# A whole program ordered by count: layer 0's weight products planned behind the last scattered rows, nine counted durations corrected, new ranks

## The chip, the core and the metric

The kernel runs on one core of a Trainium2 chip. The core has engines that run their own instruction streams side by side: PE (TensorE, matmuls and transposes), DVE (VectorE), ACT (ScalarE), POOL (GpSimd) and SP (SyncE, which here only issues DMA transfers). They meet through semaphores. The metric is the device time of one execution in microseconds (us).

## What is computed

A transformer of four layers on 4 sequences ("rows") of 512 tokens with 128 features, in float32. Each layer has two half-weighted feed-forwards around an attention, and the same feed-forward weights are used twice:

```
x = x + 0.5 * ffn(layernorm(x))
x = x + attn(layernorm(x))
x = x + 0.5 * ffn(layernorm(x))
```

This change touches layer 0 most. Its feed-forward is a mixture of 8 experts, two per token, and one shared expert:

```
scores = softmax(xt @ gate_w.T)
_, idx = top_k(scores + gate_b, 2)
comb = (take_along_axis(scores, idx)[..., None] * one_hot(idx, E)).sum(1)
for each expert e:
    h = swiglu((xt @ w1[e] + b1[e]) * (xt @ w3[e] + b3[e]))
    routed += comb[:, e] * (h @ w2[e] + b2[e])
shared = swiglu((xt @ sw1 + sb1) * (xt @ sw3 + sb3)) @ sw2 + sb2
return routed + shared
```

Layer 0's attention has 16 heads of 64 with low-rank queries, keys and values and a rotary turn of queries and keys; its output is `out @ w_out.T + residual`. Layer 1's feed-forward mixes low-rank pairs of 8 experts by a gate taken from one token of each row, and its attention looks back over a window; here the window runs along the axis of the 4 rows. Layer 2 has a switch feed-forward (one expert per token, at most 64 tokens per expert and row) and causal attention with 16 heads of 8. Layer 3 has a feed-forward that mixes each token with the one before it, and full attention with 16 heads of 8.

## The kernel before

**How the order is made.** Every stage is written as Python generators ("processes"), one for each row, tile or head. A process yields a request before each piece of work: which engine, how many us it is counted at, which buffers it needs, which named events it waits for, and the earliest time. `run` keeps a counted clock for each engine. Again and again it takes the request that can start earliest; among requests of one engine that could start at nearly the same counted time, the process with the lowest number in the table RANK goes first. `any_of` and `moving` offer a choice of engines; the one that would be done first is taken, with an addition for dearer engines (DEARER0 until the second feed-forward of layer 0 has its buffers, DEARER after that, DEARER2 once the first heads of layer 2 begin). Where PE would idle in the count, `kept_warm` puts in junk matmuls on the identity (L1523). So the order of each engine's instructions is fixed when the program is built. On the chip nothing of the count remains: an engine takes its instructions in that order, and waits only for semaphores that follow from data, buffers and transfers.

**Layer 0's feed-forward, first time (0 to about 180 us).** Row by row, `route` finds the two experts of each token and the token's place among that expert's rows, which needs the counts of the rows before it. It then scatters the normalised tokens to these places in a table `sorted_x` in device memory: L631, on POOL, eight indirect DMAs for each row, 32 in all, each counted at 1.3 us. Its event `asent{b}` is the counted end of row b's last scatter plus 2.3 us. `weigh` (L643 to L650) makes the gate weights. Meanwhile PE has work that doesn't need the routing:

- `common`, the shared expert: L685 up-projections into PSUM, L1459 on ACT or DVE adds a bias, L692, L700, L705, L708, L710 and L717 form the gated value on DVE, ACT or POOL, L724 is the down-projection (16 matmuls on the profile for a row), and L728 on DVE adds it to x.
- `fold`: L738 makes room for the biases in each expert's weights, copied back by L1453. After the last, `folded` (L745, on SP) transfers the bias rows into that room.
- `l0_outputs`: two products L1199 of attention weights, 16 matmuls of 64 rows and 64 columns each in the profile, which read different quarters of the array, and L1203 (DVE) that copies them out. They are first needed in the attention, far later.

When all rows are routed, `plan` computes which tile of 128 rows belongs to which expert: L771 on POOL casts the experts' ends, L775 to L797 on DVE work out the tiles, eight transfers of zeros on SP (L803) fill up each expert's last tile, L809 on PE turns the plan and L812 on DVE makes it whole numbers, which SP and PE read into registers. `places` (L819 to L842, DVE) finds where each token's results will lie. Then `tiled` runs tile pairs of 128 rows: SP loads them (L868; the first load waits for all scatters and zero fills), PE transposes (L876), multiplies by the expert's weights (L887, two products), ACT, DVE and POOL form the gated value (L897, L907, L913, L918, L921, L923, L927), PE transposes and multiplies again (L935, L947), and SP stores (L955). `fetched` gathers each token's results (L977, indirect DMA on POOL).

**The rest.** Layer 0's attention (`l0_rotated` L1217 to L1235, `l0_scoring` L1250, `l0_weighing` L1265, `l0_valuing` L1289, `l0_adding` L1321 and L1323) runs from about 180 to 565 us. Then comes the feed-forward of layer 0 again (second tiles from about 616 us), without any folds or L1199, then layer 1 and layer 2's first feed-forward, and from about 866 us the heads of layers 2 and 3 (L2067 scores, L2083 exponentials, L2095 masks, L2109 values) with the remaining feed-forwards between them.

The line of `run` that picks the addition for a dearer engine:

```
dearer = DEARER2 if "begin0" in events else DEARER if "tiles" in events else DEARER0
```

Of the kernel before, what the change touches and what calls it, by code (L numbers as in the profile page):

```python
# [18 lines left out]
B, S, D = 4, 512, 128  # L19
# [21 lines left out]
def done(b):  # L41
# [12 lines left out]
RANK = {  # L54
    "adda": -1.39, "att0": -17.03, "att1": 2.6, "att2": -31.37, "att3": -27.46, "backa0": -27.3, "backa1": -39.8, "backa2": -37.75, "backa3": -3.37,
    "begin0": 15.63, "begin1": -9.44, "begin2": 13.19, "begin3": -8.46, "begin4": 19.37, "begin5": 46.26, "begin6": 17.84, "begin7": 38.68,
    "bringin": 46.21, "bringing": 8.27, "channels0": -7.83, "channels1": -48.04, "channels2": -33.98, "channels3": -10.84, "channels4": -83.4,
    "channels5": -55.2, "channels6": -6.12, "commona0": -2.18, "commona1": -1.54, "commona2": -13.4, "commona3": 3.84, "commonb0": -6.75,
    "commonb1": 13.93, "commonb2": 15.85, "commonb3": 20.13, "end0": 4.32, "end1": -19.31, "end2": -8.87, "end3": -33.5, "end4": -9.59, "end5": -8.7,
    "end6": 4.72, "expsa": 17.48, "fetching": -24.33, "first0": 1.49, "first1": 0.69, "first2": -7.74, "first3": 3.2, "fold0": -3.85, "fold1": 12.13,  # L60
    "fold2": -13.35, "fold3": -46.85, "fold4": -4.06, "fold5": -6.94, "fold6": -4.77, "fold7": 29.51, "folding": -79.59, "half0": -6.96,
    "half1": -4.34, "kept0": 10.41, "kept0.0": 3.74, "kept0.1": 2.38, "kept0.2": 10.73, "kept0.3": 1.02, "kept0.4": -0.44, "kept0.5": 22.23,
    "kept0.6": 24.57, "kept0.7": -10.37, "kept0.8": 40.73, "kept0.9": 48.22, "kept0.10": 23.18, "kept0.11": 9.99, "kept0.12": 0.6, "kept0.13": 9.71,
    "kept0.14": -22.33, "kept0.15": -0.06, "kept0.16": 2.86, "kept0.17": 26.78, "kept0.18": 2.62, "kept0.19": 8.71, "kept0.20": -18.45,
    "kept0.21": -13.79, "kept0.22": 42.98, "kept0.23": 8.44, "kept0.24": -2.84, "kept0.25": -21.29, "kept0.26": 38.94, "kept0.27": -18.06,
    "kept0.28": 1.29, "kept0.29": -19.57, "kept0.30": 23.52, "kept0.31": 27.06, "l1_ready": -33.26, "looked": 76.83, "looked0": 55.63,
    "looked1": 107.62, "looked2": 88.74, "looked3": 67.36, "looked4": 70.75, "looked5": 65.59, "looked6": 63.55, "masking": 17.37, "mix0": -33.39,
    "mix1": -15.62, "mix2": 1.56, "mix3": -50.5, "mix4": -23.7, "mix5": -27.69, "mix6": -55.99, "mix7": -30.78, "ones0": -43.5, "ones1": -12.11,
    "others": 28.89, "outputs": 8.15, "placesa": -10.15, "placesb": 45.04, "plana": 39.45, "planb": -6.79, "plus0": 7.25, "plus1": 30.99,
    "rot0": 5.7, "rot1": 16.46, "rot2": 26.99, "rot3": -2.01, "rot4": 0.1, "rot5": 2.62, "rot6": 4.73, "rot7": 11.49, "rot8": 40.56, "rot9": -12.44,  # L70
    "rot10": 17.51, "rot11": -39.23, "rot12": -37.85, "rot13": 15.54, "rot14": -7.75, "rot15": 5.5, "rot16": -3.26, "rot17": 14.91, "rot18": -2.48,
    "rot19": 0.55, "rot20": -6.7, "rot21": 6.92, "rot22": 7.74, "rot23": 12.78, "rot24": 15.52, "rot25": 0.78, "rot26": -4.58, "rot27": 6.38,
    "rot28": -0.8, "rot29": -2.7, "rot30": -8.6, "rot31": -12.59, "routea0": -6.93, "routea1": -3.77, "routea2": -4.6, "routea3": -82.97,
    "routeb0": -15.04, "routeb1": -20.66, "routeb2": -1.6, "routeb3.0": -35.7, "routeb3.1": -30.11, "scorea": 18.7, "scoring": 32.74, "send0": 4.01,
    "send1": -31.58, "send2": 14.86, "send3": 33.82, "send4": 40.53, "send5": 34.29, "send6": 59.05, "send7": 34.47, "start0": 7.62,
    "start1": -25.77, "start2": -5.21, "start3": 5.86, "take0": -6.04, "take1": -13.34, "take3": 22.16, "take5": 12.18, "take7": -1.16,
    "tilea0": -19.71, "tilea1": -16.33, "tilea2": -10.97, "tilea3": -11.39, "tilea4": -31.67, "tilea5": -23.9, "tilea6": -16.68, "tilea7": -15.26,
    "tilea8": -2.27, "tilea9": 8.62, "tilea10": -2.85, "tilea11": 11.3, "tilea12": 11.37, "tilea13": 26.86, "tilea14": -11.51, "tilea15": 17.87,
    "tilea16": 25.51, "tilea17": 8.65, "tilea18": -5.64, "tilea19": 15.81, "tileb0": -6.52, "tileb1": -26.02, "tileb2": -13.14, "tileb3": -7.5,
    "tileb4": -1.76, "tileb5": -15.98, "tileb6": -12.28, "tileb7": -4.02, "tileb8": 4.67, "tileb9": 6.74, "tileb10": 0.85, "tileb11": -0.27,  # L80
    "tileb12": 13.89, "tileb13": 16.56, "tileb14": 12.26, "tileb15": 9.35, "tileb16": 12.53, "tileb17": 14.26, "tileb18": 5.96, "tileb19": 25.99,
    "turning": 87.33, "valuea": -10.03, "values": 59.72, "watched0": 49.3, "watched1": 65.31, "watched2": 7.07, "watched3": 10.64, "weigha0": 56.46,
    "weigha1": 36.64, "weigha2": 27.13, "weigha3": 34.3, "weighb0": 42.98, "weighb1": -11.29, "weighb2": 6.67, "weighb3": 18.75, "weighing": 21.28,
    "whole_l2": 12.5, "whole_l3": 12.47, "zeroing": 59.35,
}
# [3 lines left out]
ARRIVALS = {"x0": 3.6, "x1": 4.5, "x2": 5.6, "x3": 6.6, "routing": 7.5, "common": 11.5, "w130": 16.5, "w131": 21.5, "aplace": 22.0, "bs": 22.5, "w2": 25.0, "b2": 25.5, "abase0": 0.0, "bbase0": 0.0, "ident": 8.0}  # L89
DEARER2 = {"PE": 0.0, "ACT": 0.2, "DVE": 0.5, "POOL": 0.2, "SP": 0.0}  # L90
DEARER = {"PE": 0.0, "ACT": 0.1, "DVE": 0.3, "POOL": 0.2, "SP": 0.0}
DEARER0 = {"PE": 0.0, "ACT": 0.0, "DVE": 0.3, "POOL": 0.5, "SP": 0.0}
# [192 lines left out]
def program(ctx: ExitStack, tc: tile.TileContext, a: dict, out: bass.AP, worst, verdict):  # L285
# [902 lines left out]
    def l0_outputs(w, pairs):  # L1188

        wvo = w["w_out"]  # L1190
        for h2 in range(2):
            yield PE(2.3, "big", wait=["pairs", "attn_w"])
            took("big")
            pw = big()
            for q in range(4):
                hp = 4 * h2 + q
                for u in range(2):
                    r = slice(64 * u, 64 * u + 64)
                    nc.tensor.matmul(pw[r, u, q * P : (q + 1) * P], lhsT=pairs[r, hp, :], rhs=w["w_out"][r, hp, :], start=True, stop=True)  # L1199
            yield DVE(1.3)  # L1200
            for u in range(2):
                r = slice(64 * u, 64 * u + 64)
                nc.vector.tensor_copy(wvo[r, 4 * h2 : 4 * h2 + 4, :].rearrange("p h d -> p (h d)"), pw[r, u, :])  # L1203
            free("big")

    def l0_rotated(n, w, head):

        b, hp = pairs0[n]
# [22 lines left out]
        for v, m, at in ((qk, 0, t0), (other, 1, None)):  # L1231
            yield DVE(1.15, at=at)
            nc.vector.tensor_tensor(v, v, rope[:, m, :].unsqueeze(1).to_broadcast([P, 2, S]), ALU.mult)
        yield DVE(1.15)
        nc.vector.tensor_tensor(qk, qk, other, ALU.add)  # L1235
# [72 lines left out]
    def l0_adding():  # L1308

        for n, (b, hp) in enumerate(pairs0):  # L1310
# [5 lines left out]
            for i in range(3):  # L1316
                half = (i + 1) // 2
                yield DVE(1.15, wait=[f"pT{n}.{i + 1}"], at=0.0)
                pT = att["pT", n, half]
# [122 lines left out]
    def PE(us, *need, **kw):  # L1442
        return ask("PE", us, need, **kw)
# [28 lines left out]
    def DVE(us, *need, **kw):  # L1472
        return ask("DVE", us, need, **kw)

    def ACT(us, *need, **kw):
        return ask("ACT", us, need, **kw)
# [109 lines left out]
    def normal(b, make, kind, ones=False, half=False, src=None, at=None, late=0.0, split=False):  # L1586
# [11 lines left out]
        if split:  # L1598
            t0 = clock.done
            k = 1.0 / math.sqrt(D)  # L1600
            yield ACT(1.75, at=clock.begun)
            junk = tiny.tile([P, D], F32, tag="junk", name="junk", bufs=1)
# [51 lines left out]
    def lora(b, w, work, wait=()):  # L1654
# [25 lines left out]
        nc.vector.tensor_scalar(rank, rank, 2.0, 0.5, ALU.is_lt, ALU.mult)  # L1680
        yield DVE(0.6, at=max(clock.done, t1))
        nc.vector.tensor_tensor(sm, ex[:, 1:2], ex[:, 2:3], ALU.add)
# [739 lines left out]
    def l2_sent(w, work, b, rooms, key, sent, kept):  # L2422
# [20 lines left out]
        sofar = little([P, NT - 1, NE], "sofar")  # L2443
        yield DVE(1.1)
        nc.vector.scalar_tensor_tensor(order, sh, 0.0, w["c_first"].unsqueeze(1).to_broadcast([P, NT, NE]), ALU.is_equal, ALU.mult)
# [16 lines left out]
        kept += [gate, islot]  # L2462
        yield DVE(0.85, at=max(t1, t2))
        nc.vector.tensor_tensor(at, m, w["c_slot0"].unsqueeze(1).to_broadcast([P, NT, NE]), ALU.mult)
# [3 lines left out]
        nc.vector.reciprocal(gate, sm)  # L2468
        yield DVE(1.15, at=max(clock.done, t3))
        nc.vector.tensor_tensor(order, before, m, ALU.mult)  # L2470
# [170 lines left out]
    def l3_ffn(b, w, get, last, halves=1):  # L2641
# [7 lines left out]
        for m in (1, 0):  # L2649
            yield DVE(1.35, f"t{m}")  # L2650
            took(f"t{m}")
# [365 lines left out]
```

## Time and profile before

| quantity | value |
|---|---|
| median of 6 runs | 1296.55 us (1294.73 to 1302.32) |
| the profiled execution's own time | 1296.42 us |
| its span, first to last instruction | 1294.6 us |
| mean granted clock of TensorE | 0.964 of full speed |
| POOL's scatters of the first feed-forward (L631): row 0's eight | from 25.02 us |
| the other 24, one after another | first begins at 44.09, last at 74.91 us |
| first load of a tile (L868) | 95.58 us |
| first expert product (L887) | 99.30 us |
| last scatter before the second tiles | 606.32 us |

Times in the trace count from the span's start. In a line of the timeline the columns are start, length, engine, line and operation with output and inputs, the number of instructions, and in brackets the idle time of that engine just before and what ended it. PE's clock is granted by the chip: at 0.5 a matmul takes twice as long. "issue" is time for which the profile shows no cause on the engine itself; "remote" is a wait whose release it could not find.

### The profile page before, as it was taken

The numbers are of one execution on the slowest core, as the hardware profiler recorded it, in microseconds if no ns is written. First come the engines' busy times: TensorE is split into PE (matmuls) and PEld (weight loads), VectorE is DVE, ScalarE is ACT, GpSimd is POOL, SyncE is SP. The second block draws the span as 40 slices with busy tenths as digits, with TensorE's granted clock in tenths as the row PEclk, the third lists the DMA queues.
The fourth block names the chain that finished last, engine by engine and source line by source line (L and its number), as shares of the span: only waits on it lengthen the run. The fifth ranks groups of instructions, "written<-read, shape, count | busy, mean of one in ns | idle before, by whom it ended". The sixth has DMA issues, their size and how long they took to land.

```text
span 1294.6 us, 20298 instructions
## 1 busy us (share of the span) xinstructions
PE 1196.1 (92%) x6976; PEld 635.3 (49%) x6976; DVE 906.5 (70%) x2275; ACT 721.7 (56%) x1145; POOL 330.1 (26%) x324
## 2 busy tenths in 40 slices
PE   7969998999999999998898888999999899999996
PEld 4434554333533434345465557784586354544333
DVE  7857687899888788957768787768734785255233
ACT  4314454664455454613345644557757687878883
POOL 3520134600020210303014446543133212031000
PEclk9979999999999999989899988879999999999998
DMA  8113212211021111103111104100011001010000
GB/s 309 36 40 110 64 60 71 82 42 56 36 80 49 41 58 49 65 1 118 56 41 52 29 27 127 45 18 17 18 53 32 15 2 32 3 41 1 9 9 12
DMA packets 64501, 65.03 MB, mean 50 GB/s; under 512 B 11650, under 2 KB 54020, under 8 KB 64004
## 3 DMA queue, kind: packets, MB, share of 16 engines
q1 hardware_dynamic: 58244, 51.04, 12.0%
q0 software_dynamic: 6144, 12.60, 3.4%
q8 instruction: 59, 0.97, 0.3%
q14 instruction: 54, 0.43, 0.1%
HBM read 29.13 MB, written 17.69 MB: 36 GB/s over the span
## 4 chain that ended last, share of the span: by engine, by line
PE 65%; DVE 12%; issue 6%; DMA 5%; ACT 5%; POOL 3%; SPq 2%; another core or an unknown queue 1%; POOLq 0%; DVEq 0%; ACTq 0%
PE big L2067 9%; PE one L2109 8%; PE one L1289 7%; PE big L1250 6%; PE big L887 6%; PE one L1652 3%; DMA yg<-sorted_y,ito 3%; PE one L947 2%; PE big L1217 2%; PE big L685 2%; PE one L1382 2%; PE big L2519 1%; PE one L2601 1%; PE one L1341 1%; PE one L2130 1%
## 5 line engine op out<-in xcount | busy, mean ns | idle before, releaser
L2083 ACT ACTIVATE pT<-big 128x1024 f32<-128x1024 f32 (+1 forms) x224 | 205.4, 964 | 56.0 <-PE big L2067 43.2
L1615 POOL TENSOR_TENSOR rs<-rs,root 128x4 f32<-128x4 f32 x50 | 57.2, 1144 | 427.7 <-DVE rs L1613 390.4
L887 PE MATMUL big<-w_w,xsT 128*128 x312 | 152.4, 616 | 4.4 <-DVE us L907 1.8
L1265 ACT ACTIVATE pT<-big 128x1024 f32<-128x1024 f32 x128 | 123.2, 1030 | 55.1 <-PE big L1250 53.6
L2067 PE MATMUL big<-qkq,qkk 32*128 32x512 f32 (+3 forms) x1024 | 131.8, 556 | 5.4 <-ACT pT L2083 3.4
L1250 PE MATMUL big<-qk 64*128 64x512 f32 x512 | 123.0, 605 | 1.8 <-DVE qk L1235 0.8
L1289 PE MATMUL one<-pT,V 128*64 128x512 f32 x512 | 120.0, 601 | 0.8 <-ACT pT L1265 0.5
L2109 PE MATMUL one<-pT,V 128*32 128x512 f32 (+3 forms) x1024 | 112.0, 524 | 1.5 <-DVE pT L2095 0.9
L631 POOL DMA_INDIRECT sorted_x<-xn,irows x64 | 73.8, 1153 | 72.7 <-DVE irows L624 37.0
L977 POOL DMA_INDIRECT yg<-sorted_y,ito x64 | 70.0, 1094 | 53.5 <-DMA xs<-sorted_x 20.8
L1323 DVE TENSOR_TENSOR sums<-sums,pT 128x1024 f32<-128x1024 f32 x64 | 78.3, 1224 | 7.3 <-ACT pT L1265 2.9
L887 PEld LDWEIGHTS big<-w_w,xsT 128*128 128x128 f32 x312 | 55.9, 196 | 53.6 <-issue 44.4
L2067 PEld LDWEIGHTS big<-qkq,qkk 32*128 32x128 f32 x1024 | 48.4, 183 | 66.2 <-issue 43.4
L1250 PEld LDWEIGHTS big<-qk 64*128 64x128 f32 x512 | 46.2, 186 | 64.1 <-issue 43.5
L685 PE MATMUL big<-xnT,w_w 128*128 128x512 f32 x128 | 62.8, 625 | 12.5 <-DVE u L692 10.6
L1289 PEld LDWEIGHTS one<-pT,V 128*64 128x64 f32 x512 | 32.7, 136 | 79.8 <-issue 65.6
L1453 ACT COPY U<-one 128x512 f32<-128x512 f32 x54 | 31.5, 584 | 68.4 <-PE one L1289 64.2
L907 DVE TENSOR_TENSOR us<-big,t1s 128x1024 f32<-128x1024 f32 (+1 forms) x40 | 47.7, 1192 | 21.2 <-PE big L887 19.7
L897 ACT COPY t1s<-big 128x1024 f32<-128x1024 f32 (+1 forms) x40 | 39.5, 988 | 40.2 <-PE big L887 37.3
L2095 DVE TENSOR_TENSOR pT<-pT,w_c_tri 128x256 f32<-128x256 f32 (+1 forms) x96 | 50.6, 548 | 10.1 <-ACT pT L2083 9.7
L921 POOL TENSOR_SCALAR us<-us 128x512 f32<-128x512 f32 (+1 forms) x26 | 19.9, 765 | 138.3 <-DVE us L907 137.6
L2109 PEld LDWEIGHTS one<-pT,V 128*32 128x32 f32 x1024 | 24.3, 109 | 58.8 <-issue 43.2
(460 smaller groups left out, 2299.4 us busy)
## 6 DMA issues: line engine op xcount, KB each, us to landing
other<-qk SPq DMA_DIRECT2D x64, 256.0 KB
xs<-sorted_x SPq DMA_DIRECT2D x78, 64.0 KB
sorted_y<-ys SPq DMA_DIRECT2D x38, 128.0 KB
w_w<-in_w SPq DMA_DIRECT2D x2, 2048.0 KB
w_l_w<-in_l_w SPq DMA_DIRECT2D x16, 256.0 KB
X<-row_x SPq DMA_DIRECT2D x8, 256.0 KB
row_y<-y SPq DMA_DIRECT2D x8, 256.0 KB
w_w<-in_w SPq DMA_DIRECT2D x1, 1152.0 KB
```

The source lines that it names most:

```text
L631: apart(nc.gpsimd.indirect_dma_start(out=sorted_x[:, :], out_offset=bass.IndirectOffsetOnAxis(ap=irows[:, b, j, t : t + 1], axis=0), in_=x ...
L685: nc.tensor.matmul(pa[:, m, :], lhsT=w["w13"][:, NE, m, odd, c * P : (c + 1) * P], rhs=xTs[b], start=True, stop=True)
L887: nc.tensor.matmul(pa[:, k, :], lhsT=xT[:, k * P : (k + 1) * P], rhs=w["w13"][:, bass.ds(e[k], 1), m].rearrange("p o a b -> p (o a b)"), s ...
L977: nc.gpsimd.indirect_dma_start(out=y, out_offset=None, in_=sorted_y[: done(b) * P, :], in_offset=bass.IndirectOffsetOnAxis(ap=ito[:, b, j, ...
L1250: nc.tensor.matmul(sT[:, u, :], lhsT=k[r, t * P : (t + 1) * P], rhs=q[r, :], start=True, stop=True)
L1265: nc.scalar.activation(pT[:, :, t % 2, :], att["sT", n, t], AF.Exp, scale=scale)
L1289: nc.tensor.matmul(po[r, :], lhsT=V[:, t, :], rhs=pT[:, u, t % 2, :], start=(t == 0), stop=(t == NT - 1), tile_position=(0, 64 * u))
L1323: nc.vector.tensor_tensor(s, s, pT[:, :, i - 1, :], ALU.add)
L1615: nc.gpsimd.tensor_tensor(rs, rs, root, ALU.pow)
L2067: nc.tensor.matmul(sT[j // 2][:, j % 2, c : c + n], lhsT=keys[k][r, t * P : (t + 1) * P], rhs=turns[k, g][r, S - n :], start=True, stop=True)
L2083: nc.scalar.activation(p[:, :, :n], sets[i][h][:, :, :n], AF.Exp, scale=scale)
L2109: nc.tensor.matmul(po[32 * j : 32 * j + 32, S - n :], lhsT=V[k % 2][:, t, NJ * g + j, :], rhs=us[i][j // 2][:, j % 2, c : c + n], start=(t ...
```

## The change

The diff has four kinds of edits, and none in what is computed:

1. `l0_outputs`: each L1199 product is counted at 1.8 us instead of 2.3, and its request waits for the four events `asent0` to `asent3` as well, the counted landing of the last scattered rows. This is a wait of the count alone.
2. Counted durations are corrected: the rotary products and sums (L1232, L1234) and the sums of exponentials (L1318) from 1.15 to 1.21 us; part of the normalisation on ACT from 1.75 to 2.1; the gate of layer 1 on DVE from 0.6 to 0.8; three routing steps of layer 2 on DVE from 1.1, 0.85 and 1.15 to 1.35, 1.08 and 1.38; the mixing of layer 3 on DVE from 1.35 to 1.6.
3. The additions for dearer engines change: DEARER2 for ACT 0.2 to 0, for DVE 0.5 to 0.2, for POOL 0.2 to 0.5; DEARER for DVE 0.3 to 0.2.
4. Nearly all numbers of RANK are new.

```diff
 RANK = {
...
-    "bringin": 46.21, "bringing": 8.27, "channels0": -7.83, "channels1": -48.04, "channels2": -33.98, "channels3": -10.84, "channels4": -83.4,
+    "bringin": -39.29, "bringing": -6.38, "channels0": -13.22, "channels1": -45.87, "channels2": -31.65, "channels3": -8.51, "channels4": -85.75,
-    "channels5": -55.2, "channels6": -6.12, "commona0": -2.18, "commona1": -1.54, "commona2": -13.4, "commona3": 3.84, "commonb0": -6.75,
+    "channels5": -51.29, "channels6": -11.95, "commona0": 31.43, "commona1": 5.6, "commona2": -1.74, "commona3": -3.35, "commonb0": -12.69,
...
-DEARER2 = {"PE": 0.0, "ACT": 0.2, "DVE": 0.5, "POOL": 0.2, "SP": 0.0}
-DEARER = {"PE": 0.0, "ACT": 0.1, "DVE": 0.3, "POOL": 0.2, "SP": 0.0}
+DEARER2 = {"PE": 0.0, "ACT": 0, "DVE": 0.2, "POOL": 0.5, "SP": 0.0}
+DEARER = {"PE": 0.0, "ACT": 0.1, "DVE": 0.2, "POOL": 0.2, "SP": 0.0}
...
-            yield PE(2.3, "big", wait=["pairs", "attn_w"])
+            yield PE(1.8, "big", wait=["pairs", "attn_w"] + [f"asent{b}" for b in range(B)])
...
-            yield DVE(1.15, at=at)
+            yield DVE(1.21, at=at)
...
-                yield DVE(1.15, wait=[f"pT{n}.{i + 1}"], at=0.0)
+                yield DVE(1.21, wait=[f"pT{n}.{i + 1}"], at=0.0)
...
-            yield ACT(1.75, at=clock.begun)
+            yield ACT(2.1, at=clock.begun)
...
-        yield DVE(0.6, at=max(clock.done, t1))
+        yield DVE(0.8, at=max(clock.done, t1))
...
-        yield DVE(1.1)
+        yield DVE(1.35)
...
-        yield DVE(0.85, at=max(t1, t2))
+        yield DVE(1.08, at=max(t1, t2))
...
-        yield DVE(1.15, at=max(clock.done, t3))
+        yield DVE(1.38, at=max(clock.done, t3))
...
-            yield DVE(1.35, f"t{m}")
+            yield DVE(1.6, f"t{m}")
```

Put side by side, the instructions that the two programs issue differ in this: 21 more junk matmuls on PE (166 program matmuls of L1523 against 145), and some operations that can run on either of two engines are on another (10 more instructions on DVE, 7 more on POOL, 17 fewer on ACT). Every other matmul is there in both, in another order.

## The prediction

> **What bounds the kernel now.** I read the page first, then the trace by stages.
>
> ```profile
> span 1294.6 us, 20298 instructions
> PE 1196.1 (92%) x6976; PEld 635.3 (49%) x6976; DVE 906.5 (70%) x2275; ACT 721.7 (56%) x1145; POOL 330.1 (26%) x324
> PE 65%; DVE 12%; issue 6%; DMA 5%; ACT 5%; POOL 3%; SPq 2%; another core or an unknown queue 1%; POOLq 0%; DVEq 0%; ACTq 0%
> ```
>
> PE (TensorE) is busy 92% of the span and holds 65% of the chain that ended last, so a reordering that removes no matmul can win at most where PE stands idle. The windows (stretch, busy time of each engine, granted clock, DMA) say where that is:
>
> ```profile
> 60.00:80.00 20.00, 6.95 (x40) 3.76 (x38) 7.00 (x21) 2.28 (x3) 12.78 (x15) 0.81 0.15 50
> 600.00:620.00 20.00, 12.02 (x43) 6.33 (x42) 17.96 (x65) 5.17 (x9) 6.00 (x7) 0.87 0.30 97
> 680.00:820.00 140.00, 122.39 (x586) 85.05 (x585) 108.12 (x319) 75.19 (x204) 71.94 (x71) 0.90 0.21 58
> 820.00:880.00 60.00, 57.27 (x434) 46.76 (x432) 45.32 (x151) 32.82 (x73) 23.67 (x21) 0.86 0.09 26
> 340.00:560.00 220.00, 219.58 (x1065) 86.29 (x1061) 182.85 (x252) 116.69 (x140) 37.36 (x29) 1.00 0.14 53
> ```
>
> The first number of each group is busy time, PE's first. Layer 0's attention (340 to 560) has nothing to give: 0.4 us idle in 220. From 680 to 880 there are 17.6 + 2.7 = 20.3 us of idle in many small pieces. The worst place is 60 to 80: PE works 6.95 us of 20. The waits of 60 to 85 and the chain name it:
>
> ```profile
> ACT u L1459 <- remote: 13.2, 1, 13.2
> PE big L685 <- DVE u L692: 10.3, 1, 10.3
> DVE x L728 <- remote: 9.3, 1, 9.3
> ...
> 65.34 13.16 another core or an unknown queue
> ```
>
> There is one core, so "remote" means that the profile found no cause. The timeline shows what lies there:
>
> ```profile
> 56.95 1.09 PE L1199 MATMUL big<-w_w_out,w_w_up_v_pairs 64*64 64x128 f32 x16
> 59.80 1.95 PE L724 MATMUL one<-w_w,h 128*128 128x128 f32 x16
> 62.91 1.39 DVE L1203 COPY w_w_out<-big 64x512 f32<-64x512 f32 x2 [1.29 <-PE one L724]
> 74.91 0.97 POOL L631 DMA_INDIRECT sorted_x<-xn,irows  x1 [0.30 <-issue]
> 74.96 0.69 DVE L728 SCALAR_TENSOR_TENSOR x<-one,x 128x512 f32<-128x512 f32 x1 [9.29 <-remote]
> 77.09 6.72 SPq L803 DMA_DIRECT2D sorted_x<-zeros  x8
> 95.58 4.55 SPq L868 DMA_DIRECT2D xs<-sorted_x  x6
> 99.30 0.98 PE L887 MATMUL big<-w_w,xsT 128*128 x1 [0.46 <-DVE at L835]
> ```
>
> L1199 ended at 58.04, but its reader L1203 began at 62.91. L724 ended at 61.75 and its reader L728 began at 74.96. Elsewhere a reader starts within some tenths of a us of its matmul. So from L1199 on, completions were told up to 13 to 15 us late, while POOL issued one scatter (L631) per 1.27 us from 44.09 to 75.88. That the two together do it is inferred: many scatters ran before 56.95 without harm, and L1199 is what came new. PE then idled 10.3 us before L685, the shared expert and the plan (L775 to L812) came late, and the row loads (L868) and first expert matmul (L887) with them.
>
> **What the change removes.** It makes the planned order put both L1199 products behind the scatters. No semaphore is added, so nothing can be queued behind a new wait on the chip; PE keeps an order written beforehand. By position, the new PE order has all folds (L738) and all shared up-projections ahead of the first L1199. Costing each line at its mean time in this trace, 63.6 us of PE work precedes that L1199 against 46.6 before; L1199 began at 56.95 with 46.6 behind it, so now no sooner than 56.95 + 17.0 = 74.0. The last scatter should end at 75.88 or about 1 us later, as 1.0 us more DVE work precedes the routing rows (32.9 against 31.9, counted alike). A late completion can then last little, and it has a cover: before the row loads, SP must issue eight zero fills (L803), which do not wait for PE. SP's order also moves the bias rows (L745) ahead of those fills; L745 waits for ACT's last fold copy. The last fold stands at 55.8 us of PE work, so about 55.8 + 10.35 = 66.2 plus the 1.01 of the copy: done 10 us before SP needs it. Without that cover, each us the fold comes after 77 would delay all tiles by one.
>
> **First part of the sum: the row loads.** Fills began at 77.09 and held SP 6.72. Layer 0's second feed-forward has the same steps without the stall, and shows the gap from the end of the fills to the loads:
>
> ```profile
> 608.35 6.17 SPq L803 DMA_DIRECT2D sorted_x<-zeros  x8
> 616.12 8.75 SPq L868 DMA_DIRECT2D xs<-sorted_x  x11
> ```
>
> 616.12 - 614.52 = 1.60. So loads at 77.09 + 6.72 + 1.60 + 1.0 = 86.4, against 95.58: -9.2. The plan on DVE (4.6 us from 89.18 to 93.97) needs only the routing rows and fits under the fills.
>
> **Second: from load to first L887.** Before, 99.30 - 95.58 = 3.72, with one pair of transposes (L876) ahead. Now two pairs are ahead, as in the second feed-forward, where L887 came at 620.72, 4.60 after the loads: +0.9. First L887 at 91.0, against 99.30: -8.3.
>
> **Third: work moved behind that start.** One row's shared down-projection (L724, 16 matmuls, 1.78 us), with DVE's L710, L717 and L728 (0.69 each), now comes among the first tiles. There PE is the bound in most of the stretch: +1.8 for PE; the DVE pieces are hidden by DVE's idle fifth (17.96 of 20 busy at worst), or cost 2.1 if they are not.
>
> **Fourth: the clock.** PE will now idle between its last shared work and the tiles. After the idle of 4 us at the second feed-forward the half clock lasted from 618.40 to 625.23, 6.83 us; after the first it lasted 3.41 (99.58 to 102.99). At half speed 3.41 more costs 1.7 if PE is full and 0.5 if it waits a third as in 600 to 620; I take +1.0. 21 more junk matmuls (L1523) sit in gaps; each took 0.12 us a pass in the row of 22 at 94.05, so 42 passes are 4.7 to 5.0 us if a gap they were meant for is gone. I take 0, since most stand where PE waits for a load. [...]
>
> **Fifth: new ranks, corrected counts, engine prices.** Instructions stay the same in kind; DVE gets 10 more, POOL 7 more, ACT 17 fewer. Eight pieces of normalisation move from ACT (L1628, 0.48 us each) to DVE (L1630, 0.34 each): 2.7 us of DVE, spread over a kernel in which DVE idles 388 us of the span; I cost them at nothing, and at +2.7 if none of that idle time covers them. The landmarks in PE work agree within 1 us from the first heads (769.3 against 768.7) to the end; between, the last tile of the second feed-forward has 5.8 us more PE work ahead (710.2 against 704.4), as shared work was drawn forward into 600 to 620, where PE had 8 us free. Nothing in the trace prices a new order. Bounds: half of the 20.3 us idle won, -10, or as much lost, +10. I take -1, near the middle, as corrected counts are the durations the trace has (L1323 took 1224 ns, counted 1.15).
>
> Sum: -8.3 + 1.8 + 1.0 - 1 = -6.5. Span 1294.6 - 6.5 = 1288.1; the profiled run took 1296.42, 1.8 more than its span, so 1289.9, say **1290**. The median of the runs shown, 1296.55, is 0.13 above the profiled run.
>
> **Rivals.** What can be told from no change is about 0.3%, 3.9 us: below 1292.7 is faster, above 1300.4 slower.
> - *Forecast*, 0.46: 1285 to 1292.7.
> - *More*, 0.14: the ranks also close a third of the idle in 680 to 880, -7: 1283, and with half of it 1280. For it: that is the largest idle left. Against it: that idle follows transfers and routing chains that no edit shortens.
> - *Eaten*, 0.20: the start is early, but tiles then wait for DVE or the later order loses 5: 1295. For it: DVE was busy 17.96 of 20 us at the second feed-forward. Against it: attention follows at a full PE.
> - *The stall moves along*, 0.11: lateness comes from L1199 alone. The second product, planned near the fills' end (about 86), would have its completions, and those of the transposes behind it, told 78.51 - 67.31 = 11.2 us late: transposes known at 97.2, first L887 about 98.5 (-0.8), and 10 us of PE idle at half clock +3.4, and term three 1.8: 1294.6 + 4.4 + 1.8 = 1301. It decides slower from about 97. For it: nothing shows L1199 without scatters. Against it: the lateness ended 2 to 3 us after the last scatter.
> - *Second feed-forward late*, 0.09: the 5.8 us ahead of its last tile is fully paid, with the half clock of its start again (+3.4) in place of the forecast's -1: 1289.9 + 10.2 = 1300.1, slower or on the edge. Against it: the heads that follow have equal work ahead.
>
> Faster 0.60; same 0.20; slower 0.20. The range 1281 to 1300.5 leaves out half of *more* and half of *moves along*, and some of *late*.
>
> **What would show it.** Right: no "remote" wait before 100; L1203's first copy within a us of its matmul; loads near 86.4; first L887 near 91; half clock around 88 to 95. Wrong: a late reader after the new L1199 place, L745 behind 77 on SP, or the first attention scores (L1250) less than 4 us earlier than before. The first L1250 minus the end tells the fifth term apart from the rest.

## The result and the profile after

The changed kernel takes 1308.72 us in the median of 20 runs (1301.15 to 1319.71), against 1296.12 of 46 runs of the kernel before beside it: ratio 1.0096, with a 95% interval of [1.0078, 1.0115], slower by 12.6 us. The profiled execution took 1313.98, 5.3 over its median. Its first L738 stands 4.6 us later than before (21.19 against 16.55), and PE ran at half clock there from 16.66 to 23.49. In a second trace of the changed kernel without that stretch (*after_again* below) the first L738 stands at 18.06, so about 3.1 of the 4.6 us are chance of this execution and 1.5 belong to the new order.

The page of the changed kernel (in all views below, rows between those shown are left out):

```profile
span 1312.2 us, 20322 instructions
PE 1205.9 (92%) x7018; PEld 646.7 (49%) x7018; DVE 913.5 (70%) x2285; ACT 713.7 (54%) x1128; POOL 337.1 (26%) x331
PE 65%; DVE 15%; issue 6%; DMA 4%; POOL 4%; ACT 3%; another core or an unknown queue 1%; SPq 1%; POOLq 0%; DVEq 0%; ACTq 0%
```

The share of the chain that the profile gives to an unknown cause is 1%, as before. DVE's share rose from 12 to 15% and POOL's from 3 to 4%; ACT's fell from 5 to 3%. PE is busy 9.8 us longer; its 42 more matmuls are all junk (L1523, 46.09 us against 40.27), 5.8 us of that. The waits of 60 to 110, where the forecast expected no "remote" (engine, tile and line, waited for, us in total, times, longest):

```profile
DVE x L728 <- remote: 12.7, 1, 12.7
ACT u L1459 <- remote: 11.2, 2, 8.2
ACT w_w L1453 <- remote: 5.6, 1, 5.6
```

The lateness (finished matmuls whose readers are let go long after) is still there. The timeline of the same kernel tells when:

```profile
67.50 1.83 PE L724 MATMUL one<-w_w,h 128*128 128x128 f32 x14 [1.07 <-DVE h L717]
...
80.16 0.98 POOL L631 DMA_INDIRECT sorted_x<-xn,irows  x1 [0.30 <-issue]
83.82 0.69 DVE L728 SCALAR_TENSOR_TENSOR x<-one,x 128x512 f32<-128x512 f32 x1 [12.66 <-remote]
83.88 1.26 ACT L1459 ACTIVATE u<-big,w_bs 128x512 f32<-128x512 f32 x2 [8.21 <-remote]
87.33 0.30 SPq L745 DMA_DIRECT2D w_w<-in_b  x1
88.45 6.21 SPq L803 DMA_DIRECT2D sorted_x<-zeros  x8
...
94.79 0.18 DVE L775 SCALAR_TENSOR_TENSOR made<-allb,off 128x32 f32<-128x32 f32 x1
95.91 1.09 PE L1199 MATMUL big<-w_w_out,w_w_up_v_pairs 64*64 64x128 f32 x16
...
99.95 0.23 DVE L812 CAST iwho<-one 1x80 int32<-1x80 f32 x1
101.67 6.19 SPq L868 DMA_DIRECT2D xs<-sorted_x  x8
106.37 1.99 PE L887 MATMUL big<-w_w,xsT 128*128 x2
```

L724 ended at 69.33; its reader L728 began at 83.82, 2.7 us after the last scatter ended (81.14). L1199 first ran at 95.91, when all was over: in this trace it cannot be what held the completions back. What stands behind came later than before: the fills at 88.45 (11.4 us later, behind L745 at 87.33), the plan on DVE at 94.79 (5.6 later), the loads at 101.67 (6.1 later) and the first expert product at 106.37 (7.1 later).

The windows, as shown of before:

```profile
60.00:80.00 20.00, 13.62 (x43) 6.40 (x41) 8.25 (x18) 3.59 (x5) 15.28 (x15) 1.00 0.15 50
340.00:560.00 220.00, 219.98 (x1072) 89.71 (x1072) 187.15 (x260) 115.91 (x140) 34.52 (x30) 1.00 0.14 53
600.00:620.00 20.00, 16.94 (x79) 10.58 (x77) 16.03 (x56) 4.90 (x9) 9.91 (x11) 0.91 0.48 155
680.00:820.00 140.00, 123.12 (x607) 82.91 (x606) 114.27 (x324) 71.74 (x192) 74.37 (x73) 0.95 0.22 60
820.00:880.00 60.00, 55.33 (x374) 46.35 (x373) 39.45 (x116) 28.26 (x71) 22.41 (x21) 0.78 0.08 22
```

PE's busy share in 60 to 80 doubled without an earlier start: it did folds and shared work ahead of time. In 600 to 620 it works 4.9 us more, but that is mostly the place of the window: from L610 to the second tiles' first L887 both kernels have the same sequence on PE, and that L887 stands at 625.84 against 620.72. Junk takes 6.21 us of the window against 2.65, the shared up-projections L685 9.24 against 6.86. The idle of 680 to 880 is 16.9 + 4.7 = 21.6 us, 1.2 more than before, though more junk now fills it; and the clock of 820 to 880 is 0.78 against 0.86.

### The profile page after: what moved, and what is told of

Read it like the earlier page. It is cut to its first block, busy times and chain, and to the rows that moved or that the text cites. A ratio compares the mean times of both kernels' runs of the same rounds, so it can differ in the third digit from the quotient of the medians.

```text
span 1312.2 us, 20322 instructions
## 1 busy us (share of the span) xinstructions
PE 1205.9 (92%) x7018; PEld 646.7 (49%) x7018; DVE 913.5 (70%) x2285; ACT 713.7 (54%) x1128; POOL 337.1 (26%) x331
## 3 DMA queue, kind: packets, MB, share of 16 engines
q1 hardware_dynamic: 58244, 51.04, 11.9%
## 4 chain that ended last, share of the span: by engine, by line
PE 65%; DVE 15%; issue 6%; DMA 4%; POOL 4%; ACT 3%; another core or an unknown queue 1%; SPq 1%; POOLq 0%; DVEq 0%; ACTq 0%
PE big L2067 9%; PE one L2109 8%; PE one L1289 7%; PE big L1250 7%; PE big L887 5%; PE one L1652 2%; PE big L685 2%; DMA yg<-sorted_y,ito 2%; PE one L2601 2%; PE big L1217 2%; PE big L2519 1%; PE one L1341 1%; PE one L2130 1%; PE one L2582 1%
## 5 line engine op out<-in xcount | busy, mean ns | idle before, releaser
L887 PE MATMUL big<-w_w,xsT 128*128 x312 | 151.3, 614 | 3.9 <-ACT xsT L1453 3.0
L2067 PE MATMUL big<-qkq,qkk 32*128 32x512 f32 (+3 forms) x1024 | 132.0, 557 | 4.4 <-ACT pT L2083 3.0
L631 POOL DMA_INDIRECT sorted_x<-xn,irows x64 | 70.4, 1099 | 74.6 <-DVE irows L624 33.7
L977 POOL DMA_INDIRECT yg<-sorted_y,ito x64 | 73.6, 1149 | 45.4 <-DMA sorted_y<-ys 24.9
L887 PEld LDWEIGHTS big<-w_w,xsT 128*128 128x128 f32 x312 | 56.3, 197 | 55.2 <-issue 45.3
L2067 PEld LDWEIGHTS big<-qkq,qkk 32*128 32x128 f32 x1024 | 49.6, 185 | 64.8 <-issue 41.6
L907 DVE TENSOR_TENSOR us<-big,t1s 128x1024 f32<-128x1024 f32 (+1 forms) x40 | 47.7, 1194 | 26.5 <-PE big L887 20.9
L685 PE MATMUL big<-xnT,w_w 128*128 128x512 f32 x128 | 63.6, 630 | 0.0
```

Source lines behind the costliest of these rows:

```text
L631: apart(nc.gpsimd.indirect_dma_start(out=sorted_x[:, :], out_offset=bass.IndirectOffsetOnAxis(ap=irows[:, b, j, t : t + 1], axis=0), in_=x ...
L685: nc.tensor.matmul(pa[:, m, :], lhsT=w["w13"][:, NE, m, odd, c * P : (c + 1) * P], rhs=xTs[b], start=True, stop=True)
L887: nc.tensor.matmul(pa[:, k, :], lhsT=xT[:, k * P : (k + 1) * P], rhs=w["w13"][:, bass.ds(e[k], 1), m].rearrange("p o a b -> p (o a b)"), s ...
L977: nc.gpsimd.indirect_dma_start(out=y, out_offset=None, in_=sorted_y[: done(b) * P, :], in_offset=bass.IndirectOffsetOnAxis(ap=ito[:, b, j, ...
L2067: nc.tensor.matmul(sT[j // 2][:, j % 2, c : c + n], lhsT=keys[k][r, t * P : (t + 1) * P], rhs=turns[k, g][r, S - n :], start=True, stop=True)
```

## The experiments

Kernels of one chip are compared with the kernel before on that chip; the chips turn out to matter. "Early" is everything up to layer 0's attention end, "late" what follows.

**1. The wait and the counts apart (chip 8).** *wait_alone* is the kernel before with the first kind of edit only:

```diff
-            yield PE(2.3, "big", wait=["pairs", "attn_w"])
+            yield PE(1.8, "big", wait=["pairs", "attn_w"] + [f"asent{b}" for b in range(B)])
```

> The kernel before with the L1199 edit alone (counted 1.8, planned behind the scattered rows); ranks, counts and prices are the old ones. Theory P (the prediction's: L1199 under running scatters is what delays PE's completions): no wait on an unknown cause above 2 us before 100 us, first L887 at 89 to 94 us, and the whole 3 to 8 us faster than before unless the changed order later eats it. Theory S (a long unbroken run of POOL's indirect DMAs holds PE's completions back, whatever PE runs): waits of 8 to 15 us on an unknown cause stay, released 2 to 3 us after the last scatter, first L887 at 97 to 102, and the whole within 6 us of before or slower.

1296.18 against 1294.53, 1.0009 [0.9977, 1.0041]: nothing. Neither theory came out whole. The "remote" waits stayed but fell to 6.7, 6.1 and 2.6, and the first L887 came at 92.2, as theory P has it; yet nothing was won. From there to the first L1217, the attention's first product, it took 90.4 us, where the kernels with the old early order take 83.9 to 86.8. An earlier first expert product is not by itself a faster kernel.

*counts_alone* is the kernel before with the corrected durations alone, *after_no_wait* the changed kernel with the L1199 line as it was:

```diff
-            yield DVE(1.15, at=at)
+            yield DVE(1.21, at=at)
...
-            yield DVE(1.35, f"t{m}")
+            yield DVE(1.6, f"t{m}")
```

> The kernel before with the nine corrected counts alone. The first 200 us should keep the order of before, since no corrected count lies there except the rotary ones: first L887 at 97 to 102. Theory O (any edit of the count shuffles thousands of near ties of an order whose ranks were fitted to the old counts): 5 to 15 us slower than before. Rival (the corrected counts are nearer to the chip and so help or do nothing): within 4 us of before or faster.

> The changed kernel with the L1199 line put back as it was (2.3, no wait for the scattered rows). If the wait itself makes the loss: within 4 us of before, 1293 to 1300. If the new ranks and prices make it: 1304 to 1313, like the changed kernel. With theory S the waits on an unknown cause before 100 us are 8 to 15 us long here too.

counts_alone took 1319.55, 1.0177 [1.0128, 1.0225], after_no_wait 1320.72, 1.0168 [1.012, 1.0216]. Both lose more than the whole change does, and more than any of the expectations said. The wait is not what makes the loss.

*no_product* is the kernel before without L1199 and L1203; it leaves the product of the attention weights out.

```diff
-            pw = big()
...
-                    nc.tensor.matmul(pw[r, u, q * P : (q + 1) * P], lhsT=pairs[r, hp, :], rhs=w["w_out"][r, hp, :], start=True, stop=True)
...
-                nc.vector.tensor_copy(wvo[r, 4 * h2 : 4 * h2 + 4, :].rearrange("p h d -> p (h d)"), pw[r, u, :])
```

> The kernel before with the 16 L1199 matmuls and the four L1203 copies left out; their requests stay in the count, so the order of all else is the same. Layer 0's attention output then uses the unmultiplied weights. Theory P: no wait on an unknown cause above 2 us before 100 us, first L887 near 88 to 92, 6 to 11 us faster than before (2.2 us of it the missing matmuls). Theory S: waits of 8 to 15 us on an unknown cause stay at 60 to 80 us, first L887 at 96 to 100, 0 to 4 us faster.

1295.71, 0.9994 [0.9958, 1.0031]. Its timeline (L1450 here is L1459 of before):

```profile
71.44 0.69 ACT L1450 ACTIVATE u<-big,w_bs 128x512 f32<-128x512 f32 x1 [10.23 <-remote]
...
75.69 0.69 ACT L1450 ACTIVATE u<-big,w_bs 128x512 f32<-128x512 f32 x1 [3.56 <-remote]
76.35 0.97 POOL L631 DMA_INDIRECT sorted_x<-xn,irows  x1 [0.30 <-issue]
79.92 0.69 ACT L1450 ACTIVATE u<-big,w_bs 128x512 f32<-128x512 f32 x1 [3.03 <-remote]
```

16.8 us of such waits without a single L1199, as theory S has it. That L1199 is the cause of the lateness is refuted.

**2. The halves, one group of ranks, and the scatters (chip 1).** *early_new* has the wait, the early counts (L1232, L1234, L1318) and new ranks of the early steps; *late_new* has the other counts, the new additions for dearer engines and new ranks of the late steps. Of the 225 ranks that change, 121 are early and 104 late; two lines of late_new's diff:

```diff
-DEARER2 = {"PE": 0.0, "ACT": 0.2, "DVE": 0.5, "POOL": 0.2, "SP": 0.0}
+DEARER2 = {"PE": 0.0, "ACT": 0, "DVE": 0.2, "POOL": 0.5, "SP": 0.0}
```

> Everything of the change that bears on layer 0's first feed-forward and attention: the L1199 edit, the three corrected counts L1232, L1234 and L1318, and the new ranks of the processes of these stages. All later ranks, counts and prices are the old ones, and by position the order from the second feed-forward on is that of before. If the loss is made late (theory L, from the changed kernel's trace: more gaps of PE from the second feed-forward's last tiles to layer 2): within 4 us of before, 1291 to 1299. If it is made early (theory E: shared work drawn ahead of the tiles, transfers of zeros behind the bias rows): 6 to 13 us slower, 1301 to 1308.

> The other half of the change: new ranks of the second feed-forward and all after it, new prices, the six other counts; L1199, the early ranks and the early counts as before. By position its order is that of before up to layer 0's attention and exactly that of the changed kernel after it. Theory L: 8 to 14 us slower than before, 1303 to 1309, the loss between the second tiles (L887) and the first heads (L2067). Theory E: within 4 us of before.

early_new took 1308.33, 1.0102 [1.0082, 1.0122], late_new 1305.53, 1.0075 [1.0046, 1.0104]. Both halves lose, so theories L and E are each half right; the sum would be 1.8%, the whole loses 0.96%.

*tile_ranks* is the changed kernel with three ranks as before:

```diff
-"tileb17": 43, "tileb18": 30.94, "tileb19": 55.13,
+"tileb17": 14.26, "tileb18": 5.96, "tileb19": 25.99,
```

> The changed kernel with the ranks of three processes put back: tileb17, tileb18 and tileb19 (the second feed-forward's last tile pairs) from 43, 30.94, 55.13 to 14.26, 5.96, 25.99. If these late tiles hold up the last row of layer 1 (theory T): the last L947 comes 5 to 14 us earlier and the whole is 4 to 9 us faster than the changed kernel, 1300 to 1305. If the gaps come from the order as a whole, single ranks do not mend it: 1305 to 1325.

1322.69, 1.0206 [1.0176, 1.0236]. The second feed-forward's last product came some 7 us earlier after its start, 164.6 against 172.1, and later stages lost more than that, so theory T is refuted.

*paused* is the kernel before with pauses, uncounted, on POOL:

```diff
+                    if key == "a" and b and (2 * t + j) % 4 == 3:
+                        idle = pool.tile([P, 128], F32, tag="idle", name="idle", bufs=1)
+                        for _ in range(10):
+                            nc.gpsimd.memset(idle, 0.0)
```

> The kernel before with ten small memsets on POOL (about 2 us, not in the count) after every fourth scatter of rows 1 to 3 of the first feed-forward, so that its run of 24 indirect DMAs is cut into runs of four; the order of all other instructions is unchanged. Theory S (an unbroken run of indirect DMAs holds PE's completions back): no wait on an unknown cause above 3 us between 50 and 95 us, though the scatters end about 13 us later, so L887 starts at 105 to 112 and the whole is 6 to 14 us slower. Rival (each indirect DMA delays them, run or not): waits of 8 to 15 us on an unknown cause again, up to the end of the scatters near 90.

1308.3, 1.0096 [1.0072, 1.012], as theory S has it: the last scatter ended at 91.30 instead of 75.88. But there is no "remote" wait from 50 to 110. Its timeline (lines behind L631 are 4 higher: L1463, L728 and L732 are L1459, L724 and L728 of before):

```profile
69.86 2.76 POOL L635 MEMSET idle<- 128x128 f32 x10
70.66 0.69 ACT L1463 ACTIVATE u<-big,w_bs 128x512 f32<-128x512 f32 x1 [1.02 <-PE big L689]
71.70 1.83 PE L728 MATMUL one<-w_w,h 128*128 128x128 f32 x14 [0.86 <-DVE h L721]
73.98 0.68 DVE L732 SCALAR_TENSOR_TENSOR x<-one,x 128x512 f32<-128x512 f32 x1
...
90.33 0.97 POOL L631 DMA_INDIRECT sorted_x<-xn,irows  x1 [0.30 <-issue]
```

The product ends at 73.53 and its reader starts at 73.98, 0.45 later, while scatters still have 18 us to go. In the trace of the kernel before a reader L728 began 13.2 us after its L724 (61.75 to 74.96). With runs of indirect DMAs cut to four the lateness is gone in this trace: here it goes with long unbroken runs of them. That the pauses themselves, and not the changed timing of all else, do it is inferred.

**3. What holds the fills (chip 3).** *after_behind* is the changed kernel with the bias transfer L745 asked for behind the zero fills; *early_cast* is the kernel before with the cast L771 moved from POOL, where it queues behind all 32 scatters, to DVE right behind the last row's base:

```diff
-            yield ask("SP", 0.1)
+            yield ask("SP", 0.1, wait=f"{key}zeroed")
```

```diff
+                if b == B - 1:
+                    found["ibase"] = kept([P, NE], "ibase", I32)[0:1, :]
+                    nc.vector.tensor_copy(found["ibase"], bases[B][0:1, :])
...
-            nc.gpsimd.tensor_copy(ibase, base[0:1, :])
+            ibase = found["ibase"]
```

*early_cast_wait* adds the first kind of edit to early_cast, and *after_behind_cast* is after_behind with early_cast's edit.

> The changed kernel, but SP issues the bias rows (L745) behind the eight zero fills instead of ahead of them; nothing else moves. In the changed kernel's trace L745 waited for the last fold's copy until 87.3 us and the fills began at 88.2. Theory F (the fills behind L745 are what holds the first tiles): fills begin within 2 us of the last scatter's end, first loads 7 to 10 us earlier against the last scatter than in the changed kernel, the whole 3 to 10 us faster than it, 1299 to 1306. Rival (the plan on DVE or the last shared work holds them anyway): loads within 2 us, the whole within 3 us of the changed kernel.

> The kernel before, but the cast of the experts' ends (L771, on POOL behind all scatters) is done on DVE right after the last row's counts are known (one instruction more behind L619), so that the zero fills need not wait for POOL's queue; the order of all else is the same. First feed-forward: fills begin 10 us or more before the last scatter's end, but the loads still wait for the plan (iwho at 94), first L887 at 97 to 100. Second feed-forward: fills begin 5 to 7 us earlier, loads when the plan is ready, 4 to 5 us earlier against the last scatter. The whole 2 to 6 us faster than before. Rival (what is won is lost again in the stages that follow): within 2 us of before.

> wait_alone with the same early cast on DVE. First L887 of the first feed-forward at 88 to 92, of the second 4 to 5 us earlier than in wait_alone against the last scatter; the whole 2 to 8 us faster than before, 1288 to 1294. Rival: within 2 us of before.

> after_behind with the early cast on DVE. Loads of the first feed-forward within 5 us of the last scatter's end, of the second 4 to 5 us earlier; the whole 6 to 14 us faster than the changed kernel, 1295 to 1303, still not faster than before, since the loss of the changed order from layer 1 on remains. Rival (the loss was all in the first feed-forward): 1288 to 1295.

The kernel before ran at 1281.39 on this chip; the changed kernel was not run here. after_behind took 1289.61, 1.0056 [1.003, 1.0081]; early_cast 1272.22, 0.9921 [0.9886, 0.9955]; early_cast_wait 1272.52, 0.9924 [0.9894, 0.9954]; after_behind_cast 1282.04, 1.0002 [0.9977, 1.0027]. None of the four traces has a "remote" wait between 40 and 112, so after_behind can't tell what L745 cost; that stays open. early_cast is faster than the kernel before, by 9.2 us, more than was expected. Its SP in the first and second feed-forward:

```profile
48.62 6.26 SPq L803 DMA_DIRECT2D sorted_x<-zeros  x8
76.30 0.32 SPq L745 DMA_DIRECT2D w_w<-in_b  x1
82.81 7.03 SPq L868 DMA_DIRECT2D xs<-sorted_x  x9
...
587.69 6.24 SPq L803 DMA_DIRECT2D sorted_x<-zeros  x8
597.41 7.85 SPq L868 DMA_DIRECT2D xs<-sorted_x  x10
```

The fills now run 28 us before the last scatter's end, and in the second feed-forward the loads follow the last scatter (593.0) by 4.4 us. In the kernel before on chip 7, which also shows no lateness, the fills' issue itself lies in that path, and the loads follow the last scatter (598.8) by 8.8:

```profile
599.83 6.16 SPq L803 DMA_DIRECT2D sorted_x<-zeros  x8
607.60 7.02 SPq L868 DMA_DIRECT2D xs<-sorted_x  x9
```

That is 4.4 us won; in the first feed-forward it is as much (the loads 4.9 us after the last scatter against 9.4), together 8.9 of the 9.2, read between two chips.

**4. Chip 7.** *early_behind* is early_new with L745 behind the fills; *late_again* repeats late_new, and *before_again* is the kernel before, unchanged.

> early_new (the early half of the change alone, 1.0 per cent slower than before) with the bias rows L745 issued behind the zero fills; nothing else differs from early_new. Theory F (L745 ahead of the fills is the whole loss of the early half): within 4 us of before, 7 to 14 us faster than early_new. Rival (the early order loses elsewhere too, as after_behind suggests, which won back only about 4): 4 to 9 us slower than before.

> The kernel before, unchanged, for a profile on the same chip as the others of this call. Within 4 us of before; the stages as in its first profile, up to 5 us each by chance of the clock.

> late_new once more. 5 to 12 us slower than before. Theory G (the new order has longer gaps of PE while rows pass one by one through the end of the second feed-forward, layer 1 and layer 2's first feed-forward): most of it between the second tiles and the first heads, with more idle or junk time of PE there than before_again. Rival: the heads of layers 2 and 3 lose most of it.

early_behind took 1285.96, 1.0038 [1.0013, 1.0063]; before_again 1282.97, 1.0006 [0.9983, 1.0028]; late_again 1293.22, 1.0101 [1.0064, 1.0137], as theory G has it. early_behind is within theory F's 4 us (1282.21 is the kernel before on this chip), but early_new ran on another chip, one with the lateness: whether L745 or the missing lateness made the difference is not told apart. The trace of before_again:

```profile
65.27 1.09 PE L1199 MATMUL big<-w_w_out,w_w_up_v_pairs 64*64 64x128 f32 x16
70.50 1.83 PE L724 MATMUL one<-w_w,h 128*128 128x128 f32 x14 [0.65 <-DVE h L717]
72.78 0.68 DVE L728 SCALAR_TENSOR_TENSOR x<-one,x 128x512 f32<-128x512 f32 x1
75.74 0.98 POOL L631 DMA_INDIRECT sorted_x<-xn,irows  x1 [0.30 <-issue]
77.81 6.19 SPq L803 DMA_DIRECT2D sorted_x<-zeros  x8
86.08 6.21 SPq L868 DMA_DIRECT2D xs<-sorted_x  x8
89.65 2.93 PE L887 MATMUL big<-w_w,xsT 128*128 x3 [0.46 <-ACT xsT L1453]
```

This is the kernel before, instruction for instruction, with L1199 in the middle of the same long run of scatters, and the readers are prompt (L724 ends at 72.33, L728 begins at 72.78). The first expert product comes at 89.65 instead of 99.30.

**5. Chip 5.** *after_again* is the changed kernel, *before_third* the kernel before, and *early_cast_again* repeats early_cast on a chip that does have the lateness.

> The changed kernel once more, beside before_third. On a chip whose trace shows no late completions: first fills within 2 us of the last scatter, first L887 at 90 to 94, and still 0.3 to 1.0 per cent slower than before, since the late order remains. On a chip that shows them: 0.7 to 1.2 per cent slower, first L887 at 100 to 107. If the loss needed the lateness: within 0.3 per cent of before on a chip without it.

> early_cast once more. 0.4 to 1.2 per cent faster than before on either kind of chip: the second feed-forward's fills begin 5 to 7 us before its scatters end, which does not depend on late completions.

> The kernel before, unchanged, for its profile on the same chip. Within 4 us of before; remote waits of 8 to 15 us before 100 us only if the chip is of the kind that takes 1294 to 1297.

after_again took 1309.52, 1.0122 [1.007, 1.0174], with its first L887 at 102.2, as expected for a chip with the lateness; early_cast_again 1293.19, 0.9979 [0.995, 1.0009], no clear gain where 0.4 to 1.2 per cent were expected; before_third 1297.78, 1.0005 [0.9961, 1.005]. In early_cast_again the fills are early too (47.78), but the plan ended at 95.38 behind held shared work, the loads came at 97.00, and the first L887 at 100.4 against 98.9 in before_third.

## Why the prediction failed

**First and second part (loads at 86.4, first L887 at 91.0, -8.3): the step that failed.** "That the two together do it is inferred: many scatters ran before 56.95 without harm, and L1199 is what came new." no_product shows the lateness without L1199, and the changed kernel shows it before L1199. On chip 8 a long run of scatters with no L1199 at all was enough (16.8 us of such waits in no_product). So the edit moved L1199 out of a stall that it did not make. First L887 came 7.1 us later in the profile, about 4.0 without the 3.1 us of chance at its start; on chip 5, where neither execution has such a stretch, it was 102.2 against 98.9, +3.3. The term was missed by about 12 us. Single traces leave 5 us open here: late_new, which has the old early order, had its first L887 at 94.53. With the lateness the sentence "the plan ... fits under the fills" failed too: in the changed kernel the plan ended at 100.18 and the loads came 1.5 us behind it, while the fills had ended at 94.66. What the lateness costs the kernel before is 99.30 - 89.65 = 9.65 us at this place, between two chips. Where it is absent the loads do follow the fills, and the start came out as worked out, first L887 at 91.6 in after_behind and 91.0 in early_behind (both with L745 behind the fills), but there the kernel before begins at 89.65 already, and nothing is won.

**The cover for L745** ("done 10 us before SP needs it") was priced without lateness, and gave way: 66.2 was forecast for the last fold; its copy was done at 87.30 and SP left L745 at 87.63. It did not set the end in this trace, as the plan did: iwho at 99.95 and loads at 101.67, with fills finished at 94.66. How much L745 alone would cost on a chip with lateness was not separated.

**Third part (+1.8): near.** From first L887 to first L1217 took 83.9 to 86.8 us with the old early order and 86.5 to 88.5 with the new; in pairs it is +0.8 (first pair) and +2.1 (chip 5). (17.96 of 20 us busy leaves DVE a tenth idle, not the fifth that the prediction reads from it.)

**Fourth part (half clock of 6.83 us after the start): right in length, 14 us later than forecast.** It lasted from 101.99 to 108.82. Its +1.0 can't be read apart: the half clock ahead of it adds up to 17.1 us in this trace and 10.2 in after_again, which has the same order.

**Fifth part (-1 within -10 to +10): wrong sign, at the bound.** The late order alone costs 1.0075 and 1.0101 on two chips, 9 to 11 us. By stretches of the traces, new order less old, in us:

| stretch | first pair of traces (before, after) | chip 5 (before_third, after_again) | chip 7, late order alone (before_again, late_again) |
|---|---|---|---|
| start to first L887 | +7.1 | +3.2 | +1.5 |
| to first L1217 | +0.8 | +2.1 | +0.4 |
| to the second tiles' first L887 | -2.8 | -7.3 | -4.8 |
| to the last L947 of that feed-forward | +13.7 | +13.2 | +16.6 |
| to first L2067 | -5.4 | -11.9 | -3.8 |
| to the end | +4.2 | +4.5 | +3.8 |
| whole span | +17.6 | +3.8 | +13.7 |

Chip 5's small total comes from a profile of the changed kernel's fastest execution (1301.75 of a median of 1309.52), so single traces don't settle the size; the medians above do. What all three pairs share is a loss of 13 to 17 us in the second feed-forward, where *Second feed-forward late* pointed with 5.8, a part of it given back in the next stretch, and some 4 us more lost in the heads.

The step that failed here is the bound. It was taken from the idle time of 680 to 880, but in the first pair the second feed-forward's 13.7 us are mostly work: from its first L887 to its last L947 PE is busy 156.41 us against 145.16. Junk takes 4.34 us where the kernel before has none, one row's shared down-projection (16 matmuls of L724, 2.3 us) and a piece of layer 1 (L1642 to L1688) stand in it that came behind it before, and idle time grew by 2.5 us. That work stands among the tiles, not in 600 to 620 as the prediction has it. One instance, the last tile, in the changed kernel:

```profile
787.46 0.68 DVE L907 TENSOR_TENSOR us<-big,t1s 128x512 f32<-128x512 f32 x1
789.20 3.51 PE L1523 MATMUL big<-w_c_ident 128*128 128x128 f32 x30
792.17 1.62 DVE L1684 SCALAR_TENSOR_TENSOR gate<-rank,ex,sm 128x1 f32<-128x1 f32 x1
793.71 0.68 DVE L927 SCALAR_TENSOR_TENSOR hs<-sgs,us 128x512 f32<-128x512 f32 x1
794.44 0.66 PE L935 MATMUL one<-w_c_ident,hs 128*128 128x128 f32 x4 [1.73 <-DVE hs L927]
795.61 0.43 DVE L927 SCALAR_TENSOR_TENSOR hs<-sgs,us 128x256 f32<-128x256 f32 x1
796.77 0.44 PE L935 MATMUL one<-w_c_ident,hs 128*128 128x128 f32 x2
```

and in the kernel before:

```profile
773.95 0.68 DVE L907 TENSOR_TENSOR us<-big,t1s 128x512 f32<-128x512 f32 x1
777.25 0.43 DVE L927 SCALAR_TENSOR_TENSOR hs<-sgs,us 128x256 f32<-128x256 f32 x1
778.21 0.38 PE L935 MATMUL one<-w_c_ident,hs 128*128 128x128 f32 x2
```

The last tile is a single one: its L907 has 128x512 numbers and its L927 128x256; the L927 of 128x512 at 793.71 belongs to the pair ahead of it. From its L907 to its L927 it takes 8.15 us against 3.30. DVE's order has layer 1's gate between (L1666 at 789.01 to L1684 at 792.17, 1.62 us long), PE fills the gap with 3.51 us of junk and then waits 1.73 more. The prediction compared PE work ahead of a landmark and saw 5.8 us here, but not the waits of the tile chain on DVE and the junk that covers them. "The heads that follow have equal work ahead" was true and no protection: work ahead is not time. Nor is this wait shown to be the loss: in tile_ranks the same tile takes 3.66 us and the whole is slower still.

**The sum.** With the runs' numbers: +3 to +4 for the start, +1 to +2 for the work behind it, +9 to +11 for the late order: +13 to +17 against +12.6 measured. That agreement should not be leaned on, since the parts don't add: the halves cost 1.02% and 0.75%, the whole 0.96%, the counts alone 1.77%. Why they don't is open; that these orders are fitted as a whole, and lose when a piece is exchanged, is a reading that tile_ranks, counts_alone and after_no_wait support and no run proves. The granted clock explains little of the loss. On chip 5 the changed kernel's runs have a mean clock of 0.965 and those of the kernel before 0.968; the time of a run multiplied by one minus its clock is 45.8 against 42.5 us in the medians, so by this estimate at most some 3 of the 15 us there.

## What to carry to other kernels

A coincidence in one trace ("L1199 is what came new") names a suspect; look for the same stall without the suspect, or run without it, before a whole term of a sum rests on it. When an order is made anew from corrected counts, idle time does not bound what it can lose: filler and work moved forward on the busiest engine cost as well, and what one landmark loses the next may give back, so only the end tells. And put an operation that others wait for ahead of a run of indirect DMAs on its engine, not behind it: that won 0.8% on one chip and nothing clear on another.

## What the hardware showed

*Completions of PE told late.* While POOL issued, in the trace of the changed kernel, a long unbroken run of indirect DMAs, one per 1.28 us, readers of finished matmuls on ACT and DVE began up to 14.5 us after them (69.33 to 83.82, 12.7 of it with DVE idle), and the last of them were let go 2.7 us after the run's end. With the runs cut to four (paused) no such wait is left. That is one trace of one kernel, and it shows that the lateness goes with the runs, not how. By what mechanism the completions are held back is open.

*Chips differ.* On chips 1, 5 and 8 the kernel before takes 1294 to 1297 us, and the traces taken there show the lateness, but for the paused kernel's; on 3 and 7 it takes 1281 to 1283, and none of the seven traces taken there has a "remote" wait between 40 and 112. The mean granted clock of the kernel before differs too, 0.967 to 0.969 against 0.972. What sets the two kinds of chip apart is not known from these runs. A scheduling experiment that passes on one kind says nothing of the lateness on the other: after_behind was lost to that.

*Half clock in pieces.* In the traces of before and after the stretches at half clock came in lengths of 3.41 us (99.58 to 102.99 in before) and its multiples, but for the last, which the span's end cuts off: twice that from 101.99 to 108.82 in after, four times from 72.27 to 85.92 in before. In after four matmuls L685 took 3.76 us at a granted clock of 0.50 (from 17.64) and 1.88 at 1.00 (from 26.22).
